# Bias network in two half-width column tiles, with the channel halves summed on VectorE and the tables made on ScalarE

## Chip, cores, metric

One core of one Trainium2 chip. The metric is device time in microseconds (us) of one execution. The kernel before takes 3495.07 us (median of 2 runs, 3491.4 to 3498.73). Engines in the profile: PE is TensorE (matmuls), PEld its weight loads, DVE VectorE, ACT ScalarE, POOL GpSimd, SP the engine that issues most transfers.

## The reference, cut to what matters

Two layers of a network; the first holds an attention whose 8 heads (times 2 images) get a bias from a small network. It runs on every pair of 1024 query points and 64 key points:

```python
pos = grid_q[:, :, None, :] - grid_kv[:, None, :, :]           # (16, 1024, 64, 2)
bias = jnp.sign(pos) * jnp.log1p(jnp.abs(pos))
bias = jax.nn.relu(bias @ cpb_w1 + cpb_b1)                      # 2 -> 128
bias = jax.nn.relu(bias @ cpb_w2 + cpb_b2)                      # 128 -> 128
bias = (bias @ cpb_w3 + cpb_b3).reshape(b, GROUPS, H * W, Hd * Wd)   # 128 -> 1
sim = jnp.einsum('bhid,bhjd->bhij', qh, kh) + bias
attn = jax.nn.softmax(sim, axis=-1)
```

After it come an output projection, an MLP, and a plain attention over 1024 points; they aren't changed. All is fp32.

## The kernel before

Two heads (a unit) are handled at a time. One step s makes 1024 positions for one j (a key point of a head): layer 1 on VectorE (`h1`, an addition of two table rows with a clamp), layer 2 as two matmul calls of 128x512 into one PSUM pair (a tile of 128x2x512), a relu on ScalarE (`h2`). After four steps layer 3 runs: four 32-column tiles at a time, one per j, into the scores `sim`. The tables come by DMA and are scaled on GpSimd, for 32 steps at once.

```python
def st_table(c):                                # 32 times
    t = lp.tile([P, 4, CJ, 64], F32, name="tab")            # 2 buffers
    nc.sync.dma_start(out=..., in_=src[...].partition_broadcast(P))   # 1 MB
    nc.gpsimd.tensor_scalar(tf[:, :, 0:32], tf[:, :, 0:32], col("w1x"), col("cb1"), ALU.mult, ALU.add)
    nc.gpsimd.tensor_scalar(tf[:, :, 32:64], tf[:, :, 32:64], col("w1y"), None, ALU.mult)
def st_layer2(s):
    ps = p2p.tile([P, 2, 512], F32, name="ps2")             # 2 buffers
    for h in range(2):
        nc.tensor.matmul(ps[:, h, :], cw2, h1[:, h * 512 : (h + 1) * 512], start=True, stop=True)
    nc.scalar.activation(h2, ps, AF.Relu, bias=col("cb2"))
def st_layer3(q):
    ...
    for h in range(2):
        for i in range(4):
            nc.tensor.matmul(sims[u, h][32 * i : 32 * i + 32, :], w3p[:, JH - 1 - jj : 2 * JH - 1 - jj],
                             h2[i][:, h, :], start=False, stop=(jj == JH - 1))
# ... softmax, projection, MLP and second attention cut
for s in range(4 * NQ + 1):                     # 1024 steps
    if s + 2 < 4 * NQ:
        st_layer1(s + 2)
    if s % (4 * CJ) == 4 * CJ - 3 and s // (4 * CJ) + 2 < NT:
        st_table(s // (4 * CJ) + 2)
    if s < 4 * NQ:
        st_layer2(s)
    if s and s % 4 == 0:
        st_layer3(s // 4 - 1)
        ...
```

The framework in which it is written puts in the semaphores, and it may also reorder instructions of an engine when it builds the program.

Of the kernel before, what the change touches and what calls it, by code (L numbers as in the profile page):

```python
# [24 lines left out]
JH = J // 2  # L25
CJ = 8
# [6 lines left out]
    ("bq", 4), ("bk", 4), ("bp", 4), ("dwb", 1), ("cb1", 1), ("cb2", 1), ("cb3", 1), ("w3", 1),  # L33
    ("dww", 36), ("w1x", 1), ("w1y", 1),
]
# [9 lines left out]
def conv_seq_kernel(ctx: ExitStack, tc: tile.TileContext, x, cst, vec, wsm, outw, w1, w2, wl, bv, out):  # L45
# [11 lines left out]
    w3p = cp.tile([P, 2 * JH - 1], F32, name="w3p")  # L57
# [13 lines left out]
    with tc.tile_pool(name="ph", bufs=1) as ph, tc.tile_pool(name="ph2", bufs=2) as ph2, tc.tile_pool(  # L71
# [33 lines left out]
        nc.gpsimd.memset(qpad[:, :, 1 : PW - 1, PW - 1], 0.0)  # L105
        nc.gpsimd.memset(w3p, 0.0)
        nc.gpsimd.tensor_copy(w3p[:, JH - 1 : JH], col("w3"))
# [99 lines left out]
        for wx, blk, sc in ((wk, kblk, DH ** (-0.5)), (wv, vblk, 1.0)):  # L207
# [6 lines left out]
            for f in range(2):  # L214
                r = slice(64 * f, 64 * f + 64)
                nc.vector.tensor_scalar(
                    blk[r, :, r].rearrange("p (b k) j -> p k b j", b=B),
                    pkk[r, :].rearrange("p (k b j) -> p k b j", k=NCH, b=B), sc, None, ALU.mult,
                )
# [44 lines left out]
    w1_s = mwp.tile([P, NCH, 4 * C], F32, name="w1_s")  # L264
    for k in range(NCH):
        nc.scalar.dma_start(out=w1_s[:, k, :], in_=w1[:, k, :])
# [3 lines left out]
    NQ = NU * JH  # L270
    with tc.tile_pool(name="lp", bufs=2) as lp, tc.tile_pool(
# [6 lines left out]
        def st_table(c):  # L278

            u, i = divmod(c, JH // CJ)  # L280
            b, k = units[u]
            t = lp.tile([P, 4, CJ, 64], F32, name="tab")
            src = fd[b * NCH + k].rearrange("f (a j) e -> (f a) (j e)", a=2)
            nc.sync.dma_start(
                out=t.rearrange("p a j e -> p a (j e)"),
                in_=src[:, i * CJ * 64 : (i + 1) * CJ * 64].partition_broadcast(P),
            )
            tf = t.rearrange("p a j e -> p (a j) e")
            nc.gpsimd.tensor_scalar(  # L289
                tf[:, :, 0:32], tf[:, :, 0:32], col("w1x"), col("cb1"), ALU.mult, ALU.add  # L290
            )
            nc.gpsimd.tensor_scalar(tf[:, :, 32:64], tf[:, :, 32:64], col("w1y"), None, ALU.mult)  # L292
            tabs[c] = t

        def st_layer1(s):
            q, i = divmod(s, 4)
            e = tabs[q // CJ][:, i, q % CJ, :]
# [7 lines left out]
            h1s[s] = h1  # L305

        def st_layer2(s):
            h1 = h1s.pop(s).rearrange("p y x -> p (y x)")
            ps = p2p.tile([P, 2, 512], F32, name="ps2")
            for h in range(2):  # L310
                nc.tensor.matmul(  # L311
                    ps[:, h, :], cw2, h1[:, h * 512 : (h + 1) * 512], start=True, stop=True
                )
            h2 = lp.tile([P, 2, 512], F32, name="h2", bufs=6)
            nc.scalar.activation(h2, ps, AF.Relu, bias=col("cb2"))  # L315
            h2s[s] = h2

        def st_layer3(q):
            u, jj = divmod(q, JH)
# [9 lines left out]
            h2 = [h2s.pop(4 * q + i) for i in range(4)]  # L329
            for h in range(2):  # L330
                for i in range(4):
                    nc.tensor.matmul(  # L332
                        sims[u, h][32 * i : 32 * i + 32, :], w3p[:, JH - 1 - jj : 2 * JH - 1 - jj],
                        h2[i][:, h, :], start=False, stop=(jj == JH - 1),
                    )

        def softmax_steps(u, h):
# [3 lines left out]
            nc.vector.tensor_scalar(ss, sim, col("cb3"), None, ALU.add)  # L341
# [4 lines left out]
            ptv = pt.rearrange("p (a j) -> p a j", j=J)  # L346
            mx = lp.tile([P, 8], F32, name="mx")
            nc.vector.tensor_reduce(mx, ptv, AX.X, ALU.max)
            ex = lp.tile([P, 8, J], F32, name="ex")
            nc.vector.tensor_tensor(ex, ptv, mx.unsqueeze(2).to_broadcast([P, 8, J]), ALU.subtract)  # L350
# [13 lines left out]
            nc.vector.tensor_copy(atts[b][:, k, h, :], pt)  # L364
# [18 lines left out]
        NT = NQ // CJ  # L383
# [5 lines left out]

        st_table(0)  # L390
        st_table(1)
        for s in range(2):
            st_layer1(s)
        for s in range(4 * NQ + 1):
            if s + 2 < 4 * NQ:
                st_layer1(s + 2)
            if s % (4 * CJ) == 4 * CJ - 3 and s // (4 * CJ) + 2 < NT:
                st_table(s // (4 * CJ) + 2)
            if s < 4 * NQ:
                st_layer2(s)  # L400
            if s and s % 4 == 0:
                q = s // 4 - 1
                st_layer3(q)
                if q % JH == JH - 1:
                    for h in range(2):
                        tails.append(softmax_steps(q // JH, h))
                        next(tails[-1])
            elif s % 4 == 2:
# [6 lines left out]
    with tc.tile_pool(name="mp", bufs=1) as mp, tc.tile_pool(name="pm", bufs=8, space=PSUM) as pm:  # L415
        w2_s = mp.tile([P, NF, C], F32, name="w2_s")
        for k in range(4):
            nc.sync.dma_start(out=w2_s[:, 4 * k : 4 * k + 4, :], in_=w2[:, 4 * k : 4 * k + 4, :])
        for b in range(B):
            for h in range(2):  # L420
# [8 lines left out]
                for i in range(NF):  # L429
                    ps = pm.tile([P, 512], F32, tag="ps", name="psh")  # L430
                    for k in range(NCH):
                        nc.tensor.matmul(  # L432
                            ps, w1_s[:, k, i * P : (i + 1) * P], xn2[:, k, :],
# [130 lines left out]
def _layout(np, inputs):  # L564
# [7 lines left out]
    def twice(v):  # L572
# [8 lines left out]
        "cb2": L0["cpb_b2"].reshape(P, 1), "cb3": np.broadcast_to(L0["cpb_b3"].reshape(1, 1), (P, 1)),  # L581
        "w3": L0["cpb_w3"].reshape(P, 1), "dww": dww,
# [47 lines left out]
```

## Time and profile before

| | kernel before |
|---|---|
| time | 3495.07 us |
| span of the profiled run, mean granted TensorE clock | 3488.3 us, 0.989 |
| TensorE, VectorE, ScalarE, GpSimd busy | 97%, 43%, 37%, 5% |
| loop of the bias network: from one layer 3 to the next | 8.92 us, 256 times |

A busy share of 97% says that TensorE is the bound; the groups by shape say where; and the start times of layer 3 in the timeline give a period that can be compared over the whole loop. I use that period as the main measure. The lines are in the prediction.

### The profile page before, as it was taken

The page shows a single profiled execution, that of the slowest core. Times are in us where ns is not written, and L with a number is a line of the kernel's source. Part 1 is how long each engine was busy: PE and PEld are TensorE (multiplying, and loading weights), DVE is VectorE, ACT ScalarE, POOL GpSimd, SP SyncE. Part 2 cuts the span into 40 slices and gives each one's busy share as a digit, 9 for nine tenths or more (in the row PEclk, how much of TensorE's full clock was granted, in tenths as well). Part 3 has the DMA queues.
Part 4 walks back from the last instruction along what each step waited for, and adds up shares of the span by engine and source line. Part 5 has one row for each costly group of instructions (what it writes and reads, how often), then busy time and mean ns, then how long its engine had stood idle before and what let it go on. Part 6 is the DMA issues. An engine that isn't in the chain of part 4 may idle for free.

```text
span 3488.3 us, 28328 instructions
## 1 busy us (share of the span) xinstructions
PE 3398.3 (97%) x11132; PEld 1365.4 (39%) x11132; DVE 1508.2 (43%) x1417; ACT 1287.4 (37%) x1237; POOL 172.5 (5%) x77
## 2 busy tenths in 40 slices
PE   8589999999999999999999999999989999999999
PEld 2333333333333333333333333333334444444444
DVE  3455565555556556455655655555510000022030
ACT  1345455445444444345445455454410011010110
POOL 0010000100001000000100010000000000000000
PEclk9799999999999999999999999999999999999999
DMA  1020000100010000001000000000010000100000
GB/s 66 26 75 12 13 13 12 25 12 13 13 22 16 12 13 13 12 13 25 13 13 13 13 25 13 13 13 13 1 48 0 0 0 0 48 0 12 12 0 24
DMA packets 24242, 59.18 MB, mean 17 GB/s; under 512 B 2416, under 2 KB 2800, under 8 KB 22448
## 3 DMA queue, kind: packets, MB, share of 16 engines
q1 hardware_dynamic: 22336, 51.58, 5.5%
q10 hardware_dynamic: 1696, 5.53, 0.4%
q8 instruction: 91, 1.49, 0.2%
q0 software_dynamic: 80, 0.26, 0.0%
q14 instruction: 39, 0.32, 0.0%
HBM read 52.91 MB, written 4.46 MB: 16 GB/s over the span
## 4 chain that ended last, share of the span: by engine, by line
PE 97%; DVE 1%; DMA 1%; ACT 1%; issue 0%; POOL 0%; SPq 0%; ACTq 0%; DVEq 0%
PE ps L311 52%; PE sim L332 14%; PE psh L432 6%; PE psm L440 6%; PE psp L468 3%; PE psa L530 3%; PE pss L488 3%; PE pc L148 2%; PE pso L375 2%; PE psf L538 2%; PE psv L477 2%; PE pkv L197 0%; PE psq L122 0%; PE psx L507 0%; DMA w_s<-in_w 0%; PE sim L324 0%
## 5 line engine op out<-in xcount | busy, mean ns | idle before, releaser
L311 PE MATMUL ps<-h,cw 128*128 128x512 f32 x4096 | 1835.1, 599 | 15.0 <-DVE h L299 15.0
L299 DVE CUSTOM_DVE_ANT_1 h<-tab 128x1024 f32<-128x1024 f32 x1024 | 1266.7, 1237 | 998.4 <-PE ps L311 979.0
L315 ACT ACTIVATE h<-ps,vs 128x1024 f32<-128x1024 f32 x1024 | 1141.8, 1115 | 1212.8 <-PE ps L311 1211.7
L311 PEld LDWEIGHTS ps<-h,cw 128*128 128x128 f32 x4096 | 754.2, 190 | 1077.7 <-issue 843.5
L332 PE MATMUL sim<-h,w3p 128*32 128x512 f32 x4096 | 493.9, 598 | 0.0
L332 PEld LDWEIGHTS sim<-h,w3p 128*32 128x32 f32 x4096 | 107.3, 109 | 348.3 <-issue 348.0
L432 PE MATMUL psh<-xn,w_s 128*128 128x512 f32 x512 | 220.5, 592 | 1.6 <-issue 1.6
L440 PE MATMUL psm<-hm,w_s 128*128 128x512 f32 x512 | 220.4, 592 | 0.0
L436 ACT ACTIVATE hm<-psh,vs 128x512 f32<-128x512 f32 x64 | 44.0, 687 | 336.4 <-PE psh L432 336.4
L289 POOL TENSOR_SCALAR tab<-tab,vs 128x1024 f32<-128x1024 f32 x32 | 52.7, 1648 | 2210.0 <-DMA tab<-fd 1837.4
L444 DVE SCALAR_TENSOR_TENSOR xs<-psm,vs,xs 128x512 f32<-128x512 f32 x16 | 12.0, 750 | 315.3 <-PE psm L440 315.3
L432 PEld LDWEIGHTS psh<-xn,w_s 128*128 128x128 f32 x512 | 97.2, 190 | 124.3 <-issue 123.9
L440 PEld LDWEIGHTS psm<-hm,w_s 128*128 128x128 f32 x512 | 97.3, 190 | 122.5 <-issue 122.5
L468 PE MATMUL psp<-xs,wl_s 128*128 128x512 f32 x256 | 112.5, 602 | 4.9 <-DMA wl_s<-in_wl 4.9
L292 POOL TENSOR_SCALAR tab<-tab,vs 128x1024 f32<-128x1024 f32 x32 | 115.8, 3619 | 0.0
L488 PE MATMUL pss<-ks,qs 128*128 128x512 f32 x256 | 112.2, 592 | 0.0
L530 PE MATMUL psa<-aT,vt 128*128 128x512 f32 x256 | 111.5, 596 | 0.0
L481 DVE TENSOR_TENSOR vt<-psv,bvb 128x512 f32<-128x512 f32 x16 | 11.1, 691 | 161.0 <-PE psv L477 161.0
L543 DVE SCALAR_TENSOR_TENSOR res<-psf,vs,xs 128x512 f32<-128x512 f32 x16 | 12.0, 750 | 153.7 <-PE psf L538 153.7
L468 PEld LDWEIGHTS psp<-xs,wl_s 128*128 128x128 f32 x256 | 49.4, 194 | 67.8 <-issue 67.8
L530 PEld LDWEIGHTS psa<-aT,vt 128*128 128x128 f32 x256 | 49.0, 192 | 60.8 <-issue 60.8
L488 PEld LDWEIGHTS pss<-ks,qs 128*128 128x128 f32 x256 | 47.7, 190 | 55.5 <-issue 55.5
(105 smaller groups left out, 844.6 us busy)
## 6 DMA issues: line engine op xcount, KB each, us to landing
tab<-fd SPq DMA_DIRECT2D x32, 1024.0 KB, 8.1
xs<-in_x SPq DMA_DIRECT2D x8, 512.0 KB, 8.6
w_s<-in_w ACTq DMA_DIRECT2D x4, 1024.0 KB, 14.8
w_s<-in_w SPq DMA_DIRECT2D x4, 1024.0 KB, 7.7
wl_s<-in_wl SPq DMA_DIRECT2D x4, 1024.0 KB, 7.8
out<-res SPq DMA_DIRECT2D x16, 256.0 KB, 2.0
ow_s<-in_outw SPq DMA_DIRECT2D x1, 1024.0 KB, 4.8
ws<-in_wsm ACTq DMA_DIRECT2D x1, 960.0 KB, 9.0
```

The source lines that it names most:

```text
L148: nc.tensor.matmul(pc.rearrange("p (g y x) -> p g y x", y=8, x=8), dg, qpad[:, :, ky : ky + 29 : 4, kx : kx + 29 : 4], start=(t == 0), sto ...
L292: nc.gpsimd.tensor_scalar(tf[:, :, 32:64], tf[:, :, 32:64], col("w1y"), None, ALU.mult)
L299: nc.vector._custom_dve(TENSOR_ADD_SAT, out=h1, in0=e[:, 0:32].unsqueeze(1).to_broadcast([P, 32, 32]), in1=e[:, 32:64].unsqueeze(2).to_bro ...
L311: nc.tensor.matmul(ps[:, h, :], cw2, h1[:, h * 512 : (h + 1) * 512], start=True, stop=True)
L315: nc.scalar.activation(h2, ps, AF.Relu, bias=col("cb2"))
L332: nc.tensor.matmul(sims[u, h][32 * i : 32 * i + 32, :], w3p[:, JH - 1 - jj : 2 * JH - 1 - jj], h2[i][:, h, :], start=False, stop=(jj == JH ...
L375: nc.tensor.matmul(ps, uw[:, b * NCH + k, o * P : (o + 1) * P], at[:, k, h, :], start=(k == 0), stop=(k == NCH - 1),)
L432: nc.tensor.matmul(ps, w1_s[:, k, i * P : (i + 1) * P], xn2[:, k, :], start=(k == 0), stop=(k == NCH - 1),)
L440: nc.tensor.matmul(ps, w2_s[:, i, o * P : (o + 1) * P], hm[:, i, :], start=(i == 0), stop=(i == NF - 1),)
L468: nc.tensor.matmul(ps, wl_s[:, i, k, o * P : (o + 1) * P], xs[:, k, b, n], start=(k == 0), stop=(k == NCH - 1),)
L488: nc.tensor.matmul(ps[:, h, :], qs[:, k, t * P : (t + 1) * P], ks[:, k, h * 512 : (h + 1) * 512], start=(k == 0), stop=(k == NCH - 1),)
L530: nc.tensor.matmul(ps, vt[:, m, o * P : (o + 1) * P], aT[:, m, n], start=(m == 0), stop=(m == 7),)
```

## The change

The intent: layer 3 has 128 inputs per position and one output, so of the 32 columns that each of its instructions has (128*32 in the trace) one is of use; for that, 494 us of TensorE are busy. With the sign of the last layer's weights drawn out, both channel halves of layer 2 can be added on VectorE before layer 3, 64 sums remain, and two j fit in the 128 partitions. Layer 3 then runs half as often. Layer 2 writes 64 columns for one j and 64 for another.

```diff
-            nc.gpsimd.tensor_scalar(
-                tf[:, :, 0:32], tf[:, :, 0:32], col("w1x"), col("cb1"), ALU.mult, ALU.add
+        def st_table(c):
+            tf = tabs[c].rearrange("p a j e -> p (a j) e")
+            nc.scalar.activation(
+                tf[:, :, 0:32], tf[:, :, 0:32], AF.Identity, bias=col("cb1"), scale=col("w1x")
             )
-            nc.gpsimd.tensor_scalar(tf[:, :, 32:64], tf[:, :, 32:64], col("w1y"), None, ALU.mult)
+            nc.scalar.mul(tf[:, :, 32:64], tf[:, :, 32:64], col("w1y"))
...
+        def st_layer2(m):
+            ra = lp.tile([P, 2, 512], F32, name="ra", bufs=6)
+            rb = lp.tile([P, 2, 512], F32, name="rb", bufs=2)
+            for i, r in enumerate((ra, rb)):
+                ps = p2p.tile([P, 2, 512], F32, name="ps2")
+                for h in range(2):
+                    for f in range(2):
+                        nc.tensor.matmul(
+                            ps[64 * f : 64 * f + 64, h, :], cw2[:, 64 * i : 64 * i + 64],
+                            h1[f][:, h * 512 : (h + 1) * 512], start=True, stop=True,
+                        )
+                if i == 0:
+                    nc.scalar.activation(r, ps, AF.Relu, bias=col("cb2a"))
+                else:
+                    nc.scalar.activation(r, ps, AF.Relu, bias=magb, scale=mag)
+        def st_add(m):
+            nc.vector.scalar_tensor_tensor(ra, ra, lead, rb, ALU.mult, ALU.add)
...
-            nc.vector.tensor_scalar(ss, sim, col("cb3"), None, ALU.add)
+            nc.scalar.activation(ss, sim, AF.Identity, bias=col("cb3"))
...
-            nc.vector.tensor_copy(atts[b][:, k, h, :], pt)
+            nc.scalar.copy(atts[b][:, k, h, :], pt)
...
+        for m in range(NM + 2):                         # 512 steps, two j each
+            c, r = divmod(m, NT * CJ)                   # 16 steps per table
+            if r == 0 and 1 <= c and c + 1 < NC:
+                st_table_load(c + 1)
+            if r == NT * CJ // 2 and c + 1 < NC:        # 8 steps later
+                st_table(c + 1)
+            if m + 1 < NM:
+                st_layer1(m + 1, 0)
+            if 1 <= m <= NM:
+                st_add(m - 1)
+            if m + 1 < NM:
+                st_layer1(m + 1, 1)
+            if m < NM:
+                st_layer2(m)
...
```

Cut: the preparation of signs and weights, the new order of the keys in `kblk` and in the softmax (max and subtraction become six smaller instructions), and the MLP's first weights, now loaded in two halves.

More of the change, by code (lines that the diff above doesn't have):

```diff
@@ L24 @@
 NF = 16
-JH = J // 2
-CJ = 8
+NT = 4
+JQ = J // NT
+CJ = 4
 INF = float("inf")
@@ L32 @@
     ("bn1g", 4), ("bn1b", 4), ("bn2g", 4), ("bn2b", 4), ("outb", 4), ("mb1", 16), ("mb2", 4),
-    ("bq", 4), ("bk", 4), ("bp", 4), ("dwb", 1), ("cb1", 1), ("cb2", 1), ("cb3", 1), ("w3", 1),
+    ("bq", 4), ("bk", 4), ("bp", 4), ("dwb", 1), ("cb1", 1), ("cb3", 1),
     ("dww", 36), ("w1x", 1), ("w1y", 1),
+    ("cb2a", 1), ("cb2b", 1), ("w3a", 1), ("w3b", 1),
 ]
@@ L56, in conv_seq_kernel @@
     bns = cp.tile([P, 8], F32, name="bns")
-    w3p = cp.tile([P, 2 * JH - 1], F32, name="w3p")
+    w3p = cp.tile([P, 3 * JQ - 1], F32, name="w3p")
+    w3c = cp.tile([P, 3], F32, name="w3c")
     fd = dp.tile([B * NCH, 2, J, 64], F32, name="fd")
@@ L105, in conv_seq_kernel @@
         nc.gpsimd.memset(qpad[:, :, 1 : PW - 1, PW - 1], 0.0)
+        sgn, mag, lead = w3c[:, 0:1], w3c[:, 1:2], w3c[:, 2:3]
+        nc.vector.tensor_scalar(sgn, col("w3b"), 0.0, 2.0, ALU.is_ge, ALU.mult)
+        nc.vector.tensor_scalar(sgn, sgn, 1.0, None, ALU.subtract)
+        nc.vector.tensor_tensor(mag, col("w3b"), sgn, ALU.mult)
+        nc.vector.tensor_tensor(lead, col("w3a"), sgn, ALU.mult)
+        magb = cp.tile([P, 1], F32, name="magb")
+        nc.vector.tensor_tensor(magb, mag, col("cb2b"), ALU.mult)
         nc.gpsimd.memset(w3p, 0.0)
-        nc.gpsimd.tensor_copy(w3p[:, JH - 1 : JH], col("w3"))
+        for f in range(2):
+            r = slice(64 * f, 64 * f + 64)
+            nc.vector.tensor_copy(w3p[r, JQ * (1 + f) - 1 : JQ * (1 + f)], sgn[r, :])
         nc.gpsimd.memset(kblk, 0.0)
@@ L215, in conv_seq_kernel @@
                 r = slice(64 * f, 64 * f + 64)
-                nc.vector.tensor_scalar(
-                    blk[r, :, r].rearrange("p (b k) j -> p k b j", b=B),
-                    pkk[r, :].rearrange("p (k b j) -> p k b j", k=NCH, b=B), sc, None, ALU.mult,
-                )
+                src = pkk[r, :].rearrange("p (k b j) -> p k b j", k=NCH, b=B)
+                for b in range(B):
+                    dst = blk[r, b * NCH : (b + 1) * NCH, :]
+                    if blk is kblk:
+                        dst = dst.rearrange("p k (t f j) -> p k t f j", t=NT, f=2)[:, :, :, f, :]
+                        nc.vector.tensor_scalar(
+                            dst, src[:, :, b, :].rearrange("p k (t j) -> p k t j", t=NT), sc, None, ALU.mult
+                        )
+                    else:
+                        nc.vector.tensor_scalar(dst[:, :, r], src[:, :, b, :], sc, None, ALU.mult)
         for g in range(B * NCH):
@@ L263, in conv_seq_kernel @@
     mwp = mw.enter_context(tc.tile_pool(name="mwp", bufs=1, side="right"))
-    w1_s = mwp.tile([P, NCH, 4 * C], F32, name="w1_s")
-    for k in range(NCH):
-        nc.scalar.dma_start(out=w1_s[:, k, :], in_=w1[:, k, :])
+    w1_s = [mwp.tile([P, NCH, 2 * C], F32, name="w1_0")]
+    nc.scalar.dma_start(out=w1_s[0], in_=w1[:, :, 0 : 2 * C])
     units = [(b, k) for b in range(B) for k in range(NCH)]
     NU = len(units)
-    NQ = NU * JH
+    NQ = NU * JQ
     with tc.tile_pool(name="lp", bufs=2) as lp, tc.tile_pool(
@@ L276, in conv_seq_kernel, with st_table_load @@
         tabs, h1s, h2s, sims, atts = {}, {}, {}, {}, {}
-        def st_table(c):
-            u, i = divmod(c, JH // CJ)
+        def st_table_load(c):
+            u, i = divmod(c, JQ // CJ)
             b, k = units[u]
-            t = lp.tile([P, 4, CJ, 64], F32, name="tab")
-            src = fd[b * NCH + k].rearrange("f (a j) e -> (f a) (j e)", a=2)
+            t = lp.tile([P, 2 * NT, CJ, 64], F32, name="tab")
+            src = fd[b * NCH + k].rearrange("f (t j) e -> (f t) (j e)", t=NT)
             nc.sync.dma_start(
@@ L287, in st_table, with st_layer1 @@
             )
-            tf = t.rearrange("p a j e -> p (a j) e")
-            nc.gpsimd.tensor_scalar(
-                tf[:, :, 0:32], tf[:, :, 0:32], col("w1x"), col("cb1"), ALU.mult, ALU.add
-            )
-            nc.gpsimd.tensor_scalar(tf[:, :, 32:64], tf[:, :, 32:64], col("w1y"), None, ALU.mult)
-            tabs[c] = t
-        def st_layer1(s):
-            q, i = divmod(s, 4)
-            e = tabs[q // CJ][:, i, q % CJ, :]
+            tabs[c] = t
+        def st_table(c):
+            tf = tabs[c].rearrange("p a j e -> p (a j) e")
+            nc.scalar.activation(
+                tf[:, :, 0:32], tf[:, :, 0:32], AF.Identity, bias=col("cb1"), scale=col("w1x")
+            )
+            nc.scalar.mul(tf[:, :, 32:64], tf[:, :, 32:64], col("w1y"))
+        def st_layer1(m, f):
+            q, i = divmod(m, NT)
+            e = tabs[q // CJ][:, NT * f + i, q % CJ, :]
             h1 = lp.tile([P, 32, 32], F32, name="h1", bufs=4)
@@ L304, in st_layer1 @@
             )
-            h1s[s] = h1
-        def st_layer2(s):
-            h1 = h1s.pop(s).rearrange("p y x -> p (y x)")
-            ps = p2p.tile([P, 2, 512], F32, name="ps2")
-            for h in range(2):
-                nc.tensor.matmul(
-                    ps[:, h, :], cw2, h1[:, h * 512 : (h + 1) * 512], start=True, stop=True
-                )
-            h2 = lp.tile([P, 2, 512], F32, name="h2", bufs=6)
-            nc.scalar.activation(h2, ps, AF.Relu, bias=col("cb2"))
-            h2s[s] = h2
+            h1s[m, f] = h1.rearrange("p y x -> p (y x)")
+        def st_layer2(m):
+            h1 = [h1s.pop((m, f)) for f in range(2)]
+            ra = lp.tile([P, 2, 512], F32, name="ra", bufs=6)
[3 more added lines that the diff above has]
+                for h in range(2):
+                    for f in range(2):
+                        nc.tensor.matmul(
+                            ps[64 * f : 64 * f + 64, h, :], cw2[:, 64 * i : 64 * i + 64],
+                            h1[f][:, h * 512 : (h + 1) * 512], start=True, stop=True,
+                        )
+                if i == 0:
+                    nc.scalar.activation(r, ps, AF.Relu, bias=col("cb2a"))
+                else:
+                    nc.scalar.activation(r, ps, AF.Relu, bias=magb, scale=mag)
+            h2s[m] = ra, rb
+        def st_add(m):
+            ra, rb = h2s[m]
+            nc.vector.scalar_tensor_tensor(ra, ra, lead, rb, ALU.mult, ALU.add)
+            h2s[m] = ra
         def st_layer3(q):
-            u, jj = divmod(q, JH)
+            u, jj = divmod(q, JQ)
             b, k = units[u]
@@ L328, in st_layer3 @@
                     )
-            h2 = [h2s.pop(4 * q + i) for i in range(4)]
+            h2 = [h2s.pop(NT * q + i) for i in range(NT)]
             for h in range(2):
-                for i in range(4):
+                for i in range(NT):
                     nc.tensor.matmul(
-                        sims[u, h][32 * i : 32 * i + 32, :], w3p[:, JH - 1 - jj : 2 * JH - 1 - jj],
-                        h2[i][:, h, :], start=False, stop=(jj == JH - 1),
+                        sims[u, h][32 * i : 32 * i + 32, :], w3p[:, JQ - 1 - jj : 3 * JQ - 1 - jj],
+                        h2[i][:, h, :], start=False, stop=(jj == JQ - 1),
                     )
@@ L345, in softmax_steps @@
                 nc.tensor.transpose(pt[:, c * P : (c + 1) * P], ss[:, c * P : (c + 1) * P], ident)
-            ptv = pt.rearrange("p (a j) -> p a j", j=J)
-            mx = lp.tile([P, 8], F32, name="mx")
-            nc.vector.tensor_reduce(mx, ptv, AX.X, ALU.max)
-            ex = lp.tile([P, 8, J], F32, name="ex")
-            nc.vector.tensor_tensor(ex, ptv, mx.unsqueeze(2).to_broadcast([P, 8, J]), ALU.subtract)
+            ptv = pt.rearrange("p (a f j) -> p f a j", f=2, j=JQ)
+            mx = lp.tile([P, 2, 4], F32, name="mx")
+            ex = lp.tile([P, 8, J], F32, name="ex", bufs=1)
+            mq = lp.tile([P, 2, 16], F32, name="mq")
+            for f in range(2):
+                nc.vector.tensor_reduce(mq[:, f, :], ptv[:, f, :, :], AX.X, ALU.max)
+                nc.vector.tensor_reduce(
+                    mx[:, f, :], mq[:, f, :].rearrange("p (c t) -> p c t", t=NT), AX.X, ALU.max
+                )
+            exv = ex.rearrange("p (c f) (t j) -> p c f t j", f=2, t=NT)
+            for f in range(2):
+                nc.vector.tensor_tensor(
+                    exv[:, :, f, :, :], ptv[:, f, :, :].rearrange("p (c t) j -> p c t j", t=NT),
+                    mx[:, f, :].unsqueeze(2).unsqueeze(3).to_broadcast([P, 4, NT, JQ]), ALU.subtract,
+                )
             nc.scalar.activation(ex, ex, AF.Exp)
@@ L381, in softmax_steps @@
                     )
-        NT = NQ // CJ
+        NC = NQ // CJ
+        NM = NQ * NT
         tails = []
@@ L388, in advance @@
                 tails.pop(0)
+        st_table_load(0)
+        st_table_load(1)
         st_table(0)
-        st_table(1)
-        for s in range(2):
-            st_layer1(s)
-        for s in range(4 * NQ + 1):
-            if s + 2 < 4 * NQ:
-                st_layer1(s + 2)
-            if s % (4 * CJ) == 4 * CJ - 3 and s // (4 * CJ) + 2 < NT:
-                st_table(s // (4 * CJ) + 2)
-            if s < 4 * NQ:
-                st_layer2(s)
-            if s and s % 4 == 0:
-                q = s // 4 - 1
-                st_layer3(q)
-                if q % JH == JH - 1:
+        st_layer1(0, 0)
+        st_layer1(0, 1)
+        for m in range(NM + 2):
[12 more added lines that the diff above has]
+                st_layer2(m)
+            q, r = divmod(m - 1, NT)
+            if r == 0 and q >= 1:
+                st_layer3(q - 1)
+                if q % JQ == 0:
                     for h in range(2):
-                        tails.append(softmax_steps(q // JH, h))
+                        tails.append(softmax_steps(q // JQ - 1, h))
                         next(tails[-1])
-            elif s % 4 == 2:
+            elif r % 2 == 1:
                 advance()
@@ L415, in conv_seq_kernel @@
     with tc.tile_pool(name="mp", bufs=1) as mp, tc.tile_pool(name="pm", bufs=8, space=PSUM) as pm:
+        w1_s.append(mp.tile([P, NCH, 2 * C], F32, name="w1_1"))
+        nc.sync.dma_start(out=w1_s[1], in_=w1[:, :, 2 * C : 4 * C])
         w2_s = mp.tile([P, NF, C], F32, name="w2_s")
@@ L432, in conv_seq_kernel @@
                         nc.tensor.matmul(
-                            ps, w1_s[:, k, i * P : (i + 1) * P], xn2[:, k, :],
+                            ps, w1_s[i // 8][:, k, (i % 8) * P : (i % 8 + 1) * P], xn2[:, k, :],
                             start=(k == 0), stop=(k == NCH - 1),
@@ L580, in _layout @@
         "dwb": twice(L0["off_dw_b"].reshape(DH, 1)), "cb1": L0["cpb_b1"].reshape(P, 1),
-        "cb2": L0["cpb_b2"].reshape(P, 1), "cb3": np.broadcast_to(L0["cpb_b3"].reshape(1, 1), (P, 1)),
-        "w3": L0["cpb_w3"].reshape(P, 1), "dww": dww,
+        "cb2a": twice(L0["cpb_b2"][:64, None]), "cb2b": twice(L0["cpb_b2"][64:, None]),
+        "w3a": twice(L0["cpb_w3"][:64]), "w3b": twice(L0["cpb_w3"][64:]),
+        "cb3": np.broadcast_to(L0["cpb_b3"].reshape(1, 1), (P, 1)),
+        "dww": dww,
         "w1x": L0["cpb_w1"][0].reshape(P, 1), "w1y": L0["cpb_w1"][1].reshape(P, 1),
```

## The prediction

> **What bounds the kernel now.** I read the page first: engine shares, then the chain of work that ended last.
>
> ```profile
> PE 3398.3 (97%) x11132; PEld 1365.4 (39%) x11132; DVE 1508.2 (43%) x1417; ACT 1287.4 (37%) x1237; POOL 172.5 (5%) x77
> ...
> PE 97%; DVE 1%; DMA 1%; ACT 1%; issue 0%; POOL 0%; SPq 0%; ACTq 0%; DVEq 0%
> ```
>
> TensorE is the chain. 52% of the span is layer 2 of the bias network (line 311) and 14% layer 3 (line 332). The groups by shape give the durations that I need:
>
> ```profile
> L311 PE MATMUL ps<-h,cw 128*128 128x512 f32 x4096 | 1835.1, 599 | 15.0 <-DVE h L299 15.0
> L299 DVE CUSTOM_DVE_ANT_1 h<-tab 128x1024 f32<-128x1024 f32 x1024 | 1266.7, 1237 | 998.4 <-PE ps L311 979.0 <-POOL tab L292 19.3
> L315 ACT ACTIVATE h<-ps,vs 128x1024 f32<-128x1024 f32 x1024 | 1141.8, 1115 | 1212.8 <-PE ps L311 1211.7
> L332 PE MATMUL sim<-h,w3p 128*32 128x512 f32 x4096 | 493.9, 598 | 0.0
> L289 POOL TENSOR_SCALAR tab<-tab,vs 128x1024 f32<-128x1024 f32 x32 | 52.7, 1648 | 2210.0 <-DMA tab<-fd 1837.4
> L241 DVE SCALAR_TENSOR_TENSOR lner<-u,ab 128x1024 f32<-128x1024 f32 x1 | 1.2, 1215 | 0.0
> ```
>
> Each fp32 matmul call is two instructions (4096 against 2048 calls). Layer 2 shows 1835/4096 = 0.448 us of busy time per instruction; layer 3, whose four 32-column tiles run side by side, 494/4096 = 0.121. VectorE and ScalarE wait for TensorE a thousand times each; TensorE waits for them once, at the start. The timeline shows one period of the loop:
>
> ```profile
> 1503.76 1.93 PE L332 MATMUL sim<-h,w3p 128*32 128x512 f32 x16
> 1505.61 7.13 PE L311 MATMUL ps<-h,cw 128*128 128x512 f32 x16
> 1512.67 1.92 PE L332 MATMUL sim<-h,w3p 128*32 128x512 f32 x16
> ```
>
> From one layer 3 to the next are 8.91 us: 1.85 of layer 3 until layer 2 starts, and 7.06 of layer 2. The weight loads inside layer 2 come every 0.43 us, so 16 instructions are 6.88, and the remaining 2.03 belong to layer 3: four slots of 0.43 and some 0.3 for going into the 32-column mode and out of it. 256 periods make 2281 us.
>
> [...] 16 instructions of 592 ns in 1.92 us, and the 0.3 us above. [...] 1215 ns for a 128x1024 scalar_tensor_tensor at line 241, 687 to 746 for most 128x1024 tensor_scalar. [...] three 1.23 us instructions in 3.49 us, so one each 1.13:
>
> ```profile
> 185.00 3.49 DVE L299 CUSTOM_DVE_ANT_1 h<-tab 128x1024 f32<-128x1024 f32 x3
> ```
>
> [...] Line 315 with one takes 1115, forms without one 1040, so I take 1.2 us for the new relu with bias and scale pointers (an estimate).
>
> **The change part by part.** One step m now handles two of the old ones.
>
> *Layer 2* keeps its TensorE time. Per m it is 8 calls of 64 columns instead of 4 of 128. If the two column tiles run side by side, as four do in layer 3, they take 4 x 2 slots of 0.43 = 3.44 us, what two old steps took (2 x 1.72).
>
> *Layer 3* halves: the sum of the two channel halves packs two j into 128 partitions, so 128 groups of 8 calls instead of 256. A period of four m is now 4 x 3.44 + 2.05 = 15.81 us; 128 of them 2024. Against 2281 that removes 257 us, the whole intended gain.
>
> *The sum* is new on VectorE: 512 scalar_tensor_tensor of 128x1024, 1.22 us each, 625 us busy. Per m VectorE now has two h1 of 1.23 and one sum of 1.22: 3.38 us back to back with the overlap, beside 3.44 of TensorE. That fits by a hair, but there are waits inside. h1 has four buffers, thus two per m: the h1 of step m+1 can begin only when layer 2 of m-1 is done, which the trace shows 0.17 us after the next stream has started. The sum sits between the two h1 and waits for the second relu. With time 0 at the start of layer 2 of the first m after a layer 3:
> - that layer 2 is done at 3.61; first h1 of m+2 starts; relu (0.05 + 1.2) and semaphore end at 4.91, where h1 ends its slot at 4.74: the sum starts at 4.91, the second h1 at 6.03, and it ends at 7.26. With a semaphore and a weight load of 0.15 layer 2 can run at 7.46. TensorE was ready at 6.88: a stall of 0.58.
> - next m: VectorE starts at 7.16, the sum at 8.35 (after its relu), the second h1 ends at 10.70; TensorE is ready at 7.46 + 3.44 = 10.90: no stall. Then layer 3 gives 2 us of slack back.
> So 0.58 per period, 128 x 0.58 = +74 us.
>
> *Tables on ScalarE*: 32 times two ACTIVATEs, some 2.2 us, at a step where ScalarE has 1.0 us free between its relus. The relu after them is late by 1.1, and it frees the PSUM pair (two buffers) that layer 2 of the next m wants; of this some 0.9 reaches TensorE: +28 us. On the other side, the slowing of h1 while GpSimd works (1.65 against 1.23 in the timeline) goes, but it was hidden.
>
> *Softmax*: two moves to ScalarE (16 x 0.74 and 16 x 0.68 off VectorE), but max and subtraction become six smaller instructions, some 2.0 us for 1.37. They wait for transposes and stand ahead of the next h1. Half of these steps fall where layer 3 follows and hides them. For one (b,k) I count 2.4 + 0.2 + 0.9 + 0.75 = 4.2 us, where the transposes cost TensorE 4 x 0.54 = 2.2 before; times 8 is +17. Output projection inside the loop +3.
>
> *Rest*: the first table no longer shares the queues with 4 MB of MLP weights but with 2: -4 at the start of the loop (TensorE waits 15 us there). The kblk and vblk copies in smaller pieces: +2. The second half of the MLP weights (2 MB, 7.7 us per 1 MB) is needed 27 us into the MLP, the second layer's weights after 55: hidden, 0.
>
> Sum: -257 + 74 + 28 + 17 + 3 - 4 + 2 = -137. 3495 - 137 = **3358 us**, 3.9% faster.
>
> **The rivals.** *Column pairs don't run side by side.* Then layer 2 takes up to 512 x 3.44 = 1761 us more, some 5100. For it: pairs of 64 columns run nowhere in this kernel (line 197 works on one tile at a time). Against: layer 3 shows four tiles with four different moving operands at almost full rate. *VectorE becomes the bound*: without the overlap of its instructions, 3.68 us a step against 3.44; the same walk gives stalls of about 0.92 per period, 118 instead of 74, and longer softmax stalls: some 3410. For it: the sums carry waits that the trace of before never shows between two busy VectorE instructions. Against: the overlap is also there between different instructions in the timeline. *The waits are all hidden*, because TensorE starts the first tile of a pair while the second still waits, and ScalarE is quick enough: then only -257 and small terms count, 3250. For it: VectorE's sum is 3.38, under 3.44. Against: with two h1 pairs it can't run ahead, and each step goes TensorE, ScalarE, VectorE, TensorE.
>
> **Range and chances.** The centre is the walk, 3358. The low end, 3285, takes away half of the 122 us of stalls and a little; the high end, 3430, adds the VectorE rival and 20 us for unknown waits. Faster by over 2% means under 3425: 0.87. Within 2%: 0.08. Slower: 0.05, nearly all of it the first rival.
>
> **What would show it right or wrong.** Layer 3's busy time about 247 us; layer 2's slots still 0.43 with groups of 8 in 3.44; a period from layer 3 to layer 3 of 16.4 us on average, 15.8 at best; a new wait of layer 2 on h1, 60 to 90 us, in only one of four m; waits on the relus around the tables of about 1 us each; VectorE busy near 2120 us (63%), ScalarE 1425, GpSimd next to nothing; everything after the loop unchanged within 5 us. A period of 15.8 would say that stalls were overrated; one over 17 that VectorE's walk is longer than I think; a layer 2 that is busy 3500 us, the first rival.

Cut, where marked, are general rules about the hardware that were stated beside the traces; the numbers that stood with them are this trace's own: layer 3's 16 instructions overlap, a 128x1024 instruction with two tensors takes 1215 ns, and three VectorE instructions in a row overlap. The 1.2 us for the new relu is an estimate from the 1115 and 1040 ns (lines 315 and 187). So are the small times in the walk: 0.05 from the relu's start after h1's (0.06 in the timeline) and from the semaphores of line 311 (median 51 ns), 0.15 from the 64-column weight loads of line 197 (156 ns on average). The counts under softmax are estimates too, from instructions of 683 to 739 ns (lines 341 to 364).

## The result

3433.65 us (median of 2 runs, 3430.22 to 3437.09) against 3495.07: ratio 0.9831, interval 0.9802 to 0.986. That is 1.7% faster, under the 2% line, and 3.7 us above my range.

The page after, engine shares and the chain that ended last with its shares by line:

```profile
PE 3257.5 (95%) x13180; PEld 1143.4 (33%) x13180; DVE 2022.8 (59%) x1972; ACT 1416.1 (41%) x1333; POOL 4.2 (0%) x12
...
PE 79%; DMA 8%; DVE 7%; issue 4%; ACT 2%; SPq 0%; ACTq 0%; DVEq 0%
PE ps L339 40%; DMA tab<-fd 7%; PE sim L368 7%; PE psh L489 6%; PE psm L497 6%; DVE h L322 3%; PE psa L587 3%; PE psp L525 3%; PE pss L545 3%; DVE ra L351 2%; PE pc L162 2%; PE pso L421 2%; PE psf L595 2%; PE psv L534 2%; ACT rb L346 1%
```

The surprise stands in the chain: the load of the table (`tab<-fd`), which was hidden before, holds 7% of the span. The groups by shape (busy us, mean ns, then the idle time before and what ended it):

```profile
L339 PE MATMUL ps<-h,cw 128*64 128x512 f32 x8192 | 1864.5, 606 | 102.7 <-ACT rb L346 87.9 <-DVE h L322 11.2 <-ACT ra L344 3.6
L351 DVE SCALAR_TENSOR_TENSOR ra<-ra,w3c,rb 128x1024 f32<-128x1024 f32 x512 | 654.4, 1278 | 80.6 <-ACT rb L346 80.6
L346 ACT ACTIVATE rb<-ps,magb,w3c 128x1024 f32<-128x1024 f32 x512 | 615.8, 1203 | 325.1 <-PE ps L339 325.0
L368 PE MATMUL sim<-ra,w3p 128*32 128x512 f32 x2048 | 290.6, 605 | 0.8 <-DVE ra L351 0.8
L312 ACT ACTIVATE tab<-tab,vs 128x1024 f32<-128x1024 f32 x32 | 39.7, 1240 | 114.3 <-DMA tab<-fd 108.3 <-DVE h L322 6.0
```

Layer 2 has about the busy time of before (1864 against 1835 us), so its column pairs do run side by side. TensorE waits 88 us for the second relu, where I had expected a wait on h1, and ScalarE's table instructions wait 108 us for their load, 30 times. An undisturbed period in the timeline is as short as the 15.81 us that I had estimated for TensorE alone, and e3, without the sum, will show the same 15.74:

```profile
1510.91 1.92 PE L368 MATMUL sim<-ra,w3p 128*32 128x512 f32 x16
1512.77 13.95 PE L339 MATMUL ps<-h,cw 128*64 128x512 f32 x64
1526.65 1.92 PE L368 MATMUL sim<-ra,w3p 128*32 128x512 f32 x16
```

That is 15.74 us, against 2 x 8.92 before. But only 50 of the 127 periods are that short. Over the loop, from the first layer 3 to the last, 127 periods take 2252.2 us; at 15.74 each they would take 1999.0. In this excess of 253 us the gain was lost (e2 will show that 72 of it belong to softmax and projection, most of which the kernel before pays too). Here is one of the places, the timeline of all engines (start, length, engine, instruction, idle time before):

```profile
1476.01 0.36 SPq L303 DMA_DIRECT2D tab<-fd  x1
...
1479.06 1.20 ACT L346 ACTIVATE rb<-ps,magb,w3c 128x1024 f32<-128x1024 f32 x1 [0.63 <-PE ps L339]
...
1480.75 1.11 ACT L344 ACTIVATE ra<-ps,vs 128x1024 f32<-128x1024 f32 x1 [0.49 <-PE ps L339]
...
1484.67 1.24 ACT L312 ACTIVATE tab<-tab,vs 128x1024 f32<-128x1024 f32 x1 [2.81 <-DMA tab<-fd]
1485.82 1.19 ACT L346 ACTIVATE rb<-ps,magb,w3c 128x1024 f32<-128x1024 f32 x1
1486.91 1.14 ACT L315 ACTIVATE tab<-tab,vs 128x1024 f32<-128x1024 f32 x1
1487.04 1.28 DVE L351 SCALAR_TENSOR_TENSOR ra<-ra,w3c,rb 128x1024 f32<-128x1024 f32 x1 [2.19 <-ACT rb L346]
...
1487.06 3.63 PE L339 MATMUL ps<-h,cw 128*64 128x512 f32 x8 [2.92 <-ACT rb L346]
...
1490.62 1.05 PE L368 MATMUL sim<-ra,w3p 128*32 128x512 f32 x2
```

The load is issued at 1476.01, and what waits for it starts 8.66 us later. After the relus `rb` of step 16c-2 and `ra` of step 16c-1 ScalarE comes to the table instruction and waits for the load. The relu that layer 2 needs (`rb` of step 16c-1) stands behind it; so TensorE, whose PSUM pair it frees, is idle for 2.92 us. Then its next 8 instructions take 3.56 us until layer 3, where 8 in two tiles normally take 1.72. The windows view shows why (length, busy time of PE, PEld, DVE, ACT and POOL with counts, then the granted clock, the transfers' share and GB/s; the clock is 1.00 before the gap):

```profile
1484.00:1487.00 3.00, 0.14 (x2) 0.00 (x0) 0.85 (x1) 2.33 (x3) 0.00 (x0) 1.00 0.01 4
1487.00:1491.00 4.00, 3.94 (x9) 0.87 (x10) 1.57 (x2) 2.28 (x4) 0.00 (x0) 0.57 0.00 0
```

The granted clock is down to 0.57 in these 4.00 us; the trace's clock records have it at half for 3.4 us, after a gap of 2.92. It is not a single case: in the loop TensorE has 30 gaps of over 0.8 us, of 1.5 to 3.9 us, and the clock records show half clock for 3.4 or 6.8 us at 27 of them, from a point inside the gap or up to 1.2 us behind it, 119.5 us in all. The length of the gap alone doesn't decide it: a gap of 2.29 us was followed by 3.4 us of half clock, while gaps of 1.51, 2.21 and 2.33 had none after them (where a gap begins hangs on the modelled ends of matmuls). In this place layer 3 is also cut in two (2 instructions, then 14 after the next layer 2), so that TensorE goes from 128*64 to 128*32 and back once more (0.29 us in e8). The two periods together take 37.43 us for 31.48.

Where do the table instructions come from? In the program text they stand at step 16c+8, half a table after the load. In the built program's order on ScalarE (counted in the listing of instructions) the first stands between the two relus of step 16c-1, nine steps earlier, and the second behind them. The build has moved them. The load itself can't be earlier: with two table buffers it waits for the last h1 of step 16c-1, which reads the buffer that it overwrites (the trace has 30 waits of the load on `h`). So the pair of them ends up back to back, and what stands behind them on ScalarE pays for the 8.7 us between: in the place shown the relu `rb` starts at 1485.82, after the table instruction of 1484.67.

### The profile page after: what moved, and what is told of

It is laid out like the page before. It is cut to its first block, busy times and chain, and to the rows that moved or that the text cites. A ratio compares the mean times of both kernels' runs of the same rounds, so it can differ in the third digit from the quotient of the medians.

```text
span 3435.3 us, 31938 instructions
## 1 busy us (share of the span) xinstructions
PE 3257.5 (95%) x13180; PEld 1143.4 (33%) x13180; DVE 2022.8 (59%) x1972; ACT 1416.1 (41%) x1333; POOL 4.2 (0%) x12
## 3 DMA queue, kind: packets, MB, share of 16 engines
q10 hardware_dynamic: 1648, 3.43, 0.3%
q8 instruction: 105, 1.72, 0.2%
## 4 chain that ended last, share of the span: by engine, by line
PE 79%; DMA 8%; DVE 7%; issue 4%; ACT 2%; SPq 0%; ACTq 0%; DVEq 0%
PE ps L339 40%; DMA tab<-fd 7%; PE sim L368 7%; PE psh L489 6%; PE psm L497 6%; DVE h L322 3%; PE psa L587 3%; PE psp L525 3%; PE pss L545 3%; DVE ra L351 2%; PE pc L162 2%; PE pso L421 2%; PE psf L595 2%; PE psv L534 2%; ACT rb L346 1%
## 5 line engine op out<-in xcount | busy, mean ns | idle before, releaser
L339 PE MATMUL ps<-h,cw 128*64 128x512 f32 x8192 | 1864.5, 606 | 102.7 <-ACT rb L346 87.9
L322 DVE CUSTOM_DVE_ANT_1 h<-tab 128x1024 f32<-128x1024 f32 x1024 | 1208.3, 1219 | 371.9 <-PE ps L339 356.4
L339 PEld LDWEIGHTS ps<-h,cw 128*64 128x64 f32 x8192 | 580.3, 138 | 1350.2 <-issue 801.7
L344 ACT ACTIVATE ra<-ps,vs 128x1024 f32<-128x1024 f32 x512 | 569.5, 1112 | 585.8 <-PE ps L339 585.8
L346 ACT ACTIVATE rb<-ps,magb,w3c 128x1024 f32<-128x1024 f32 x512 | 615.8, 1203 | 325.1 <-PE ps L339 325.0
L351 DVE SCALAR_TENSOR_TENSOR ra<-ra,w3c,rb 128x1024 f32<-128x1024 f32 x512 | 654.4, 1278 | 80.6 <-ACT rb L346 80.6
L368 PE MATMUL sim<-ra,w3p 128*32 128x512 f32 x2048 | 290.6, 605 | 0.8 <-DVE ra L351 0.8
L489 PE MATMUL psh<-xn,w 128*128 128x512 f32 x512 | 220.5, 592 | 1.3 <-issue 1.3
L497 PE MATMUL psm<-hm,w_s 128*128 128x512 f32 x512 | 220.4, 592 | 0.0
L489 PEld LDWEIGHTS psh<-xn,w 128*128 128x128 f32 x512 | 97.2, 190 | 124.1 <-issue 123.4
L368 PEld LDWEIGHTS sim<-ra,w3p 128*32 128x32 f32 x2048 | 58.3, 109 | 226.6 <-issue 224.9
L545 PE MATMUL pss<-ks,qs 128*128 128x512 f32 x256 | 112.2, 592 | 0.0
```

The source lines that it names most:

```text
L322: nc.vector._custom_dve(TENSOR_ADD_SAT, out=h1, in0=e[:, 0:32].unsqueeze(1).to_broadcast([P, 32, 32]), in1=e[:, 32:64].unsqueeze(2).to_bro ...
L339: nc.tensor.matmul(ps[64 * f : 64 * f + 64, h, :], cw2[:, 64 * i : 64 * i + 64], h1[f][:, h * 512 : (h + 1) * 512], start=True, stop=True,)
L344: nc.scalar.activation(r, ps, AF.Relu, bias=col("cb2a"))
L346: nc.scalar.activation(r, ps, AF.Relu, bias=magb, scale=mag)
L351: nc.vector.scalar_tensor_tensor(ra, ra, lead, rb, ALU.mult, ALU.add)
L489: nc.tensor.matmul(ps, w1_s[i // 8][:, k, (i % 8) * P : (i % 8 + 1) * P], xn2[:, k, :], start=(k == 0), stop=(k == NCH - 1),)
```

## The experiments

**Theory A**: the loss is ScalarE's wait for a load that has only just been issued, passed on to TensorE and made longer by the clock. **Rival B**: the 2.3 us of table work on ScalarE are too much for two PSUM buffers, whenever they run. **Rival C**: VectorE, 3.47 us a step against TensorE's 3.44, is the new limit. The kernel before was run in the same rounds each time (medians 3493.58 for e1 to e4, 3494.77 for e5 to e8).

### e1: the tables where the text has them

```diff
-            nc.scalar.activation(
+            tc.keep_in_program_order(nc.scalar.activation(
                 tf[:, :, 0:32], tf[:, :, 0:32], AF.Identity, bias=col("cb1"), scale=col("w1x")
-            )
-            nc.scalar.mul(tf[:, :, 32:64], tf[:, :, 32:64], col("w1y"))
+            ))
+            tc.keep_in_program_order(nc.scalar.mul(tf[:, :, 32:64], tf[:, :, 32:64], col("w1y")))
```

The call adds an edge for the order only, no wait.

> The changed kernel, with one thing altered: the two table instructions are kept behind ScalarE's relus of step m = 16c+7, where the program has them, some 31 us after the table's load is issued; the build had moved them up to step 16c-1, right behind the issue. Theory A (ScalarE stands in its in-order queue waiting for the load to land, 8.7 us, then TensorE waits for a relu and comes back at half clock): a table costs TensorE about 1 us instead of 6 to 7, so 30 x 5.5 = 165 us go, about 3270 us; the wait of the table instructions on the load (108 us) goes to 0, the granted clock goes from 0.97 back to 0.99. Rival B (the 2.3 us of table work on ScalarE are themselves too much for two PSUM buffers): the table periods stay at 20 us and more and the time within 30 us of 3434. Rival C (VectorE, 3.47 of each 3.44 us, is what limits): again little change.

Measured: 3271.29 us, ratio to before 0.9365 (0.935 to 0.9381). The clock is 0.988. The table instructions now run where ScalarE has a moment, without a wait:

```profile
1344.63 1.20 ACT L346 ACTIVATE rb<-ps,magb,w3c 128x1024 f32<-128x1024 f32 x1 [0.63 <-PE ps L339]
1345.74 1.23 ACT L312 ACTIVATE tab<-tab,vs 128x1024 f32<-128x1024 f32 x1
1346.87 1.13 ACT L315 ACTIVATE tab<-tab,vs 128x1024 f32<-128x1024 f32 x1
1347.91 1.10 ACT L344 ACTIVATE ra<-ps,vs 128x1024 f32<-128x1024 f32 x1
```

Two periods around a table take 12.30 + 19.75 = 32.05 us for 31.48: 0.6 us per table (my prediction had 0.9). Not all of this is the relu that comes late. In the built e1, layer 3 is cut in two at 30 of the 31 tables in the loop, mostly with 8 instructions before a layer 2 and 8 after it (in e2 nowhere):

```profile
283.65 1.36 PE L368 MATMUL sim<-ra,w3p 128*32 128x512 f32 x8
...
284.93 3.65 PE L339 MATMUL ps<-h,cw 128*64 128x512 f32 x16
...
288.52 1.06 PE L368 MATMUL sim<-ra,w3p 128*32 128x512 f32 x8
...
289.51 12.67 PE L339 MATMUL ps<-h,cw 128*64 128x512 f32 x58
```

The first visit takes 1.28 us until layer 2 starts, behind a relu that the tables delayed, and the second 0.99, so about 0.3 is the late relu and about 0.3 the second visit (an estimate, which fits the price that e8 finds). The whole loop, from the first layer 3 to the last, first in the changed kernel and then in e1, in the order of the windows view above:

```profile
208.87:2461.08 2252.21, 2162.78 (x10333) 656.92 (x10331) 1820.21 (x1651) 1258.24 (x1115) 0.00 (x0) 0.97 0.07 15
207.81:2298.63 2090.82, 2090.82 (x10332) 650.80 (x10331) 1815.28 (x1651) 1257.91 (x1117) 0.00 (x0) 1.00 0.07 16
```

TensorE's 89.4 us of idle time are gone, and so is the half clock. Nothing but the order of instructions changed (ScalarE's by the edit, and where TensorE cuts layer 3 by the build), and 162 us went (3433.65 to 3271.29, in different rounds, with the kernel before within 2 us in both). Rivals B and C are out as the cause of the loss.

### e2: the tables on GpSimd again

```diff
-            nc.scalar.activation(
-                tf[:, :, 0:32], tf[:, :, 0:32], AF.Identity, bias=col("cb1"), scale=col("w1x")
+            nc.gpsimd.tensor_scalar(
+                tf[:, :, 0:32], tf[:, :, 0:32], col("w1x"), col("cb1"), ALU.mult, ALU.add
             )
-            nc.scalar.mul(tf[:, :, 32:64], tf[:, :, 32:64], col("w1y"))
+            nc.gpsimd.tensor_scalar(tf[:, :, 32:64], tf[:, :, 32:64], col("w1y"), None, ALU.mult)
```

> The changed kernel with the tables made on GpSimd again, as before. Theory A: the wait leaves ScalarE's queue as well, so 30 x 6.5 = 195 us go, but GpSimd slows the VectorE instructions beside it for some 5.5 us per table (1.65 against 1.23 in the kernel before), and VectorE now has no slack: +1.5 to 2 us per table, 50 us back; about 3290. Rival B: all of it goes, 3240. Rival C: no gain or slower than 3434, since VectorE is slowed further.

Measured: 3255.14 us, ratio 0.9317 (0.9303 to 0.9331). The wait left ScalarE's queue, and the table periods are 15.74 us like the rest: no table costs TensorE anything. My 50 us for a slowed VectorE were wrong. It is GpSimd that gets slower, by far: 7793 ns on average for 1648 (the row of the kernel before stands in the prediction; no run shows what slows it). VectorE's sums take 1307 ns on average for 1278, and its h1 keep a median of 1217. The group of the table's first half in e2:

```profile
L312 POOL TENSOR_SCALAR tab<-tab,vs 128x1024 f32<-128x1024 f32 x32 | 249.4, 7793 | 1803.2 <-DMA tab<-fd 1529.6 <-DVE h L322 273.5
```

VectorE does stand still for up to 2.0 us some 31 times without a wait that the profile shows ("issue", 58.6 us in all), but no period is longer for it. GpSimd has the time: nobody needs the table for half a chunk.

This kernel serves as the clean reference: its loop has an excess of 71.7 us over 127 periods of 15.74, from softmax and projection alone. In the changed kernel it was 253.2. So the tables cost 181.5 us there, 6.05 for each of the 30 that waited.

### e3: without the sum (wrong)

```diff
-            nc.vector.scalar_tensor_tensor(ra, ra, lead, rb, ALU.mult, ALU.add)
```

(On top of e1.)

> e1 without the 512 sums on VectorE (layer 3 reads ra alone; the result is wrong on purpose). It measures what the sum costs TensorE by itself. The clean period from layer 3 to layer 3 in the changed kernel is 15.74 us, as short as TensorE's own 15.8, so my prediction's lag of 0.58 us per period isn't there: if that holds, dropping the sum takes only the softmax and projection stalls, 10 to 40 us off e1. If VectorE limits (rival C), 70 us or more.

Measured: 3255.8 us, one run, 15 less than e1. The clean periods are the same 15.74; those with softmax get shorter (18.40 for 19.58, and 21.03 for 22.05), those at a table by 0.09. So 512 instructions of 1.28 us, 654 us of VectorE, cost TensorE some 15. The check of the result passed all the same; presumably the bias is too small for the comparison to miss half of it. It doesn't vouch for the sum, then; the order of the arithmetic in the other kernels is the change's own.

### e4: neighbouring calls on one tile

```diff
-                for h in range(2):
-                    for f in range(2):
+                for f in range(2):
+                    for h in range(2):
```

(On top of e1.)

> e1 with the two loops of layer 2 exchanged: both 512-column halves of one column tile first, then both of the other, so that neighbouring calls are on the same tile. It asks what the side-by-side run of the pairs rests on. If TensorE takes up work for another tile over at most a call or two, layer 2 loses a good part of the overlap: between 1.3 and 2 times 3.44 us per m, 500 to 1700 us more than e1. If it looks ahead far enough over the whole group, the time is that of e1 within 30 us.

Measured: 3280.39 us, one run, 9 more than e1; the clean period is 15.79 for 15.74. So the side-by-side run doesn't hang on alternating the tiles call by call: four instructions in a row on one tile (two calls) leave it whole. The build kept this order: in the built program all 1024 groups have two calls on one tile, then two on the other. The rest of the 9 us I don't explain.

### e5: one relu later

```diff
-            if r == NT * CJ // 2 and c + 1 < NC:
+            if r == 0 and 1 <= c and c + 1 < NC:
                 st_table(c + 1)
```

(On top of e1, with the second table made before the loop, as the build of the changed kernel has it.) The tables now stand behind the second relu of step 16c-1 and not in front of it, right after the load was issued as before.

> Tables on ScalarE as in the changed kernel, but kept at step 16c, one relu later in ScalarE's order than the changed kernel has them (there they stand between the two relus of step 16c-1), not nine steps later as in e1. Theory A (the wait for the load that was just issued is what costs, and then the half clock): in the changed kernel's trace the load lands 8.7 us after its issue, 2.2 us after the relu that now goes first could have started, so that relu no longer waits for the load, and the table instructions wait 1 us at most. TensorE is then held up by about 1.0 to 1.5 us per table instead of 6: 3255 + 31 x 1.3 = 3295, between 3275 and 3315. Rival B (ScalarE's time for the tables) is already out by e1; if the place in the step or the position in the chunk mattered rather than the load, this would stay within 40 us of 3434.

Measured: 3292.23 us, ratio 0.9424 (0.9409 to 0.944), where I had worked out 3295. The excess of the loop is 112.2 us, 40.5 more than e2, 1.3 per table (layer 3 cut in two as in e1 included). The wait is there, but it holds up nobody for long:

```profile
1397.08 1.20 ACT L346 ACTIVATE rb<-ps,magb,w3c 128x1024 f32<-128x1024 f32 x1 [0.63 <-PE ps L339]
1399.22 1.24 ACT L312 ACTIVATE tab<-tab,vs 128x1024 f32<-128x1024 f32 x1 [0.94 <-DMA tab<-fd]
1400.36 1.14 ACT L315 ACTIVATE tab<-tab,vs 128x1024 f32<-128x1024 f32 x1
```

One place in the queue is worth 141 us (3433.65 to 3292.23, different rounds). The loss follows what stands behind the wait, as theory A has it.

### e6: VectorE in the order of the walk

The prediction's 74 us of lag were for the order first h1, sum, second h1. The build has h1, h1, sum. On top of e2:

```diff
+            i1 = nc.vector._custom_dve(...)
+            if f == 1:
+                tc.keep_in_program_order(i1)
...
-            nc.vector.scalar_tensor_tensor(ra, ra, lead, rb, ALU.mult, ALU.add)
+            tc.keep_in_program_order(
+                nc.vector.scalar_tensor_tensor(ra, ra, lead, rb, ALU.mult, ALU.add)
+            )
```

> e2 with VectorE held to the order that the program writes down and that my prediction's walk used: first h1, the sum, second h1. The build of the changed kernel has h1, h1, sum instead. If the walk was right for its order, TensorE is short of the second h1 once per period by some 0.6 us: 128 x 0.6 = 75 us more than e2, 3330, with periods of 16.3 us and not 15.74. If the walk's waits are hidden anyhow (TensorE's queue, the relus), the time is that of e2 within 15 us.

Measured: 3315.79 us, ratio 0.949 (0.9476 to 0.9504), 61 more than e2. The clean period is 16.34; the walk gives 15.81 + 0.58 = 16.39. The walk's single stall is to be seen as well: the sum of the second m waits for its relu, and the second h1 behind it is late.

```profile
1508.73 1.28 DVE L354 SCALAR_TENSOR_TENSOR ra<-ra,w3c,rb 128x1024 f32<-128x1024 f32 x1
1509.93 2.35 DVE L322 CUSTOM_DVE_ANT_1 h<-tab 128x1024 f32<-128x1024 f32 x2
...
1512.66 1.28 DVE L354 SCALAR_TENSOR_TENSOR ra<-ra,w3c,rb 128x1024 f32<-128x1024 f32 x1 [0.38 <-ACT rb L348]
1513.86 2.35 DVE L322 CUSTOM_DVE_ANT_1 h<-tab 128x1024 f32<-128x1024 f32 x2
```

The two sums are 3.93 us apart here, not 3.47. So the walk was right, for an order that the built kernel doesn't have. With h1, h1, sum both inputs of layer 2 are ready 2.4 us after VectorE starts, and the sum, which nobody needs soon, does the waiting.

### e7: two softmax steps back on VectorE

```diff
-            nc.scalar.activation(ss, sim, AF.Identity, bias=col("cb3"))
+            nc.vector.tensor_scalar(ss, sim, col("cb3"), None, ALU.add)
...
-            nc.scalar.copy(atts[b][:, k, h, :], pt)
+            nc.vector.tensor_copy(atts[b][:, k, h, :], pt)
```

(On top of e2.)

> e2 with the two softmax steps that the change moved to ScalarE (the bias on the scores and the copy of the transposed weights, 16 each) back on VectorE. If VectorE is as tight as 3.47 of 3.44 us suggests, 16 x 1.4 = 22 us more VectorE work cost TensorE 10 to 25 us. If layer 3's two microseconds per period soak it up, the time is that of e2 within 8 us.

Measured: 3258.77 us, ratio 0.9327 (0.9313 to 0.9341); e2 has 0.9317 (0.9303 to 0.9331), in other rounds. The intervals overlap: this part of the change is worth a few us at most.

### e8: layer 3 for two groups at once

```diff
-            ra = lp.tile([P, 2, 512], F32, name="ra", bufs=6)
+            ra = lp.tile([P, 2, 512], F32, name="ra", bufs=10)
...
-            if r == 0 and q >= 1:
+            if r == 0 and q >= 2 and q % 2 == 0:
+                st_layer3(q - 2)
                 st_layer3(q - 1)
```

(On top of e2; `ss` and `ex` share two buffers and `bvb` is loaded in the last stage, to make room.)

> e2 with layer 3 done for two groups at once, every eighth step instead of every fourth (ten buffers of ra; to make room the scores and the exponentials share two buffers, and the bias of the last stage is loaded late). It asks what going into the 32-column mode and out of it costs, some 0.3 us by the trace of before: 64 of 128 goings are saved, 64 x 0.3 = 19 us, so 3236 us. If VectorE's 3.47 us per step come out once layer 3's slack is rarer, half of that or nothing.

Measured: 3230.51 us, ratio 0.9245 (0.9231 to 0.9259), the fastest here: 6% under the changed kernel, 7.5% under the one before. A double period is 31.19 us against 2 x 15.74 = 31.48:

```profile
1599.87 27.69 PE L337 MATMUL ps<-h,cw 128*64 128x512 f32 x128
1627.49 3.64 PE L366 MATMUL sim<-ra,w3p 128*32 128x512 f32 x32
1631.06 9.23 PE L337 MATMUL ps<-h,cw 128*64 128x512 f32 x42
```

0.29 us saved 64 times is 18.6 us of the 24.6 between the medians of e2 and e8 (in different rounds; the rest isn't taken apart). It is the 0.3 us for a change of tiling and back that the prediction read from the trace of before. VectorE keeps up even with layer 3's slack half as frequent.

## Why the prediction was wrong

The direction and the mechanism of the gain were right, the size was not: 3434 against 3358, outside the range. By its own terms, with the periods of the traces (us):

| term | predicted | measured | how |
|---|---|---|---|
| layer 3 halved, layer 2 unchanged | -257 | -269 | 128 x (2 x 8.92 - 15.74) |
| VectorE's lag | +74 | 0 | clean periods are TensorE's own; e6 shows +0.60 per period for the other order |
| tables on ScalarE | +28 | +181 | excess 253.2 after, 71.7 in e2 |
| softmax | +17 | +25 | 7 x (7.08 - 3.48) from the periods that hold it, e2 and before |
| projection in the loop | +3 | +3 | 4 x 7.56 - 8 x 3.43 |
| start and small copies | -2 | +7 | remainder of the spans, -53 in all; not taken apart |

**The step that failed** is "Tables on ScalarE". I wrote that the two instructions come "at a step where ScalarE has 1.0 us free between its relus" and delay the next relu by 1.1 us. That reads the place from the program text, step 16c+8, 31 us after the load. The built kernel has them at 16c-1, behind a load that is still under way. In the trace nothing on ScalarE passes them while they wait (2.81 us in the place shown, with the relu `rb` behind), so what arrives is not 2.2 us of work but the rest of 8.7 us of transfer. Of the 6.05 us per table, 2.98 are idle time (89.4 in the loop), at most 2.0 the half clock (half of the 119.5 us at that clock; in the place shown 3.56 for 1.72), and about 1.1 the split layer 3 and the rest. e1 and e5 show that the place in the queue is the cause; the share of the clock is read from the trace, and no run varies it alone. In its own place the term is 0.6, of which about half is the late relu that I had put at 0.9, and half the cut of layer 3, which I hadn't foreseen. Why the build moves them isn't settled by these runs; that it does is in the order of the built program.

**The second failure went the other way** and hid part of the first: the 74 us of lag. Again I took the order from the text, and again the build had another, this time a better one. e6 makes the walk come true within 0.05 us of its period. With both orders as written, e6's time and e1's 0.6 us for each of 31 tables would give some 3334 us, inside my range; that is an argument, no run has both.

**What was right.** Column pairs run side by side (first rival out: 1864 us busy, and e4). Layer 3's busy time in the undisturbed e2 is 248 us for 247 predicted. The relu with two pointer operands takes 1203 ns for my estimate of 1.2 us. The sum takes 1278 where I took the 1215 of a single instruction, with no effect. The MLP's second half of weights is hidden: the MLP's matmuls keep 220.5 and 220.4 us. But the stretch from the last layer 3 to the end isn't unchanged within my 5 us: it takes 974.2 for 968.0, which is in the remainder above and not taken apart. The profile of before couldn't show the order of instructions that didn't exist yet; what it could have shown is the price of a wrong place: GpSimd waited 1837 us for this very load (the row of line 289 in the prediction), and I moved its instructions into the queue of an engine that others depend on without asking what that wait would become.

## What to carry to other kernels

When an instruction that waits for a transfer moves from an idle engine to one that others wait for, ask what its wait becomes there: here the relu behind it on ScalarE paid the latency (8.66 us from the issue of the load), and TensorE lost 6.05 us per table. Find its place in the built order, not in the text, and pin it behind the landing (0.6 us per table in e1), or leave it on the idle engine (nothing in e2). The idle gaps, 2.98 us on average, cost TensorE more than their length here: at 27 of 30 the granted clock was at half for 3.4 or 6.8 us. And of two things that a busy engine makes, put first the one that the bound engine needs next: the order h1, h1, sum was worth 61 us here, for nothing.
